# Block-diagonal 128-row aggregations replaced by pairs of 64-row matmuls in a four-layer graph network

## The chip, the cores and the metric

The kernel runs on one core of a Trainium2 chip. The metric is the device time of one execution in microseconds (us); lower is better. A core has five engines [...]: TensorE (PE; its weight loads are shown apart as PEld), VectorE (DVE), ScalarE (ACT), GpSimd (POOL) and SyncE (SP), which here only starts transfers.

## The reference

There are 128 graphs of 64 nodes with 512 features each, all in f32. Four layers run one after the other; each is a residual and a layer norm around one kind of graph network:

```python
# layer 0
y = x @ w; s = y @ a
A = s[..., :, None] + s[..., None, :]
A = jnp.tanh(A / 8.0) * 8.0
A = jnp.where(A >= 0, A, 0.1 * A)
A = jnp.exp(A) * A_shape
A = A / jnp.sum(A, axis=-1, keepdims=True)
A = A * jnp.sum(A_shape, axis=-1, keepdims=True)
out = A @ x @ w
# layer 1
weight = adj * jnp.exp(einsum('bqd,bkd->bqk', query, keyt))
weight = weight / jnp.sum(weight, axis=2, keepdims=True)
out = einsum('bqk,bkd->bqd', weight, value)
# layer 2
agg = einsum('bij,bjd->bid', adj, k * mask)
w = inv_scale * mask * einsum('bid,bid->bi', q, agg)
out = softmax(w, axis=1)[:, :, None] * v
# layer 3, twice (hidden width 1024), relu and layer norm between
m = Be[:, :, None] * einsum('nce,nch->neh', H, x @ W.T)
out = Dn[:, :, None] * einsum('nce,neh->nch', H, m) + b
# after every layer
x = layernorm(x + out)
```

`H` is 1 where the adjacency is not zero, `Be` and `Dn` are inverse sums over it. Every `A @ x`-like product mixes nodes of one graph only: a 64 x 64 matrix per graph.

## The kernel before, in words

Two graphs fill the 128 partitions of a tile; a group is two such tiles (`GT = 2`), and there are 32 groups. `run(g)` is a generator that carries one group through all four layers and yields between stages; the loop at the end of the kernel keeps four groups in flight, starts one every fourth step and advances the oldest first. The framework's scheduler then sets the order within each engine's queue, so in the middle of the run a round of about 78 us repeats, in which TensorE works on four groups at different layers: layer 3's second product for the oldest, layer 2's scores, layer 1's attention, layer 0's aggregation for the youngest.

Each group's matrix of 64 x 64 per graph is spread to a 128 x 128 block-diagonal matrix per tile. The buffers for these (`e_bd` three, `h_bd` two, `g_bd` three) are zeroed once by GpSimd at the start (L90), ahead of the weights' transfers in the same queue; after that only the two diagonal blocks are written, by `on_diagonal` (L357), L425 and L461, each with two instructions of 64 partitions. With them:

- `gathered` (L282) computes the transposed aggregate of a tile with four matmuls of 128 x 128 per tile, into one PSUM buffer `tr` (there are two), which ScalarE copies to SBUF (L289); it is called in layer 0 (with `e`) and at the start of layer 3 (with `G`). Layer 3's second aggregation does the same over 1024 columns (L502, copies L503).
- `row_sums` (L324) multiplies with a column of ones, once per tile.
- Layer 1's attention is one matmul per tile (L419), and layer 3's matrix `G` one per tile (L458).

The scores of layers 1 and 2 (L320) and the broadcast of layer 0 (L374) already run as matmuls with 128 rows and 64 columns per graph, the two graphs in turn. An f32 matmul of the source is two passes in the trace, each with its own weight load.

The weight products are `product` (L296: w0, wv1, wv2, w3a, w3b) and `product_T` (L305). `transposed` (L278) transposes `x` after a layer norm, through the same two `tr` buffers; its copies are L279. The layer norm is L342 to L346 on VectorE, with its power of -0.5 on GpSimd (L335). L389, L420, L464 and L506 add a layer's result to `x`. L402 adds a bias to `x` on GpSimd.

Of the kernel before, what the change touches and what calls it, by code (L numbers as in the profile page):

```python
# [22 lines left out]
KC = D // P  # L23
KH = DH // P
# [7 lines left out]
def kernel(  # L32
# [38 lines left out]
    ones = cpool.tile([P, 1], FP, name="ones")  # L71
# [3 lines left out]
    halves = ((slice(0, N), slice(0, N)), (slice(N, P), slice(N, P)))  # L75
# [5 lines left out]

    eye = cpool.tile([P, N], FP, name="eye")
    nc.vector.tensor_add(eye, ident[:, :N], ident[:, N:])


    def diagonals(name, n):
        made = []
        for i in range(n):
            t_ = cpool.tile([P, GT, P], FP, name=f"{name}{i}")
            nc.gpsimd.memset(t_, 0.0)  # L90
            made.append(t_)
        turn = [0]

        def take():
            turn[0] += 1
            return made[turn[0] % n]

        return take

    next_e = diagonals("e_bd", 3)  # L100
    next_h = diagonals("h_bd", 2)
    next_g = diagonals("g_bd", 3)

    x_g = x.rearrange("(g t p) d -> g p t d", t=GT, p=P)
    out_g = out.rearrange("(g t p) d -> g p t d", t=GT, p=P)
# [46 lines left out]
    w3b_sb = weights(w3b, DH, D, "w3b_sb")  # L152
# [120 lines left out]
    def transposed(xt):  # L273
        xT = work.tile([P, KC, GT * P], FP, name="xT")
        for t in range(GT):
            tr = ps_tr.tile([P, KC, P], FP, name="tr")
            for c in range(KC):
                nc.tensor.transpose(tr[:, c, :], xt[:, t, ts(c, P)], ident)  # L278
            nc.scalar.copy(xT[:, :, ts(t, P)], tr)  # L279
        return xT  # L280

    def gathered(xt, bd):  # L282

        gT = work.tile([P, KC, GT * P], FP, name="xT")
        for t in range(GT):
            tr = ps_tr.tile([P, KC, P], FP, name="tr")
            for c in range(KC):
                nc.tensor.matmul(tr[:, c, :], xt[:, t, ts(c, P)], bd[:, t, :], start=True, stop=True)  # L288
            nc.scalar.copy(gT[:, :, ts(t, P)], tr)  # L289
        return gT  # L290

    def product(lhsT, t, w, cols=slice(0, D), chunks=KC):

        ps = ps_mm.tile([P, D], FP, name="mm")
        for k in range(chunks):
            nc.tensor.matmul(ps, lhsT[:, k, ts(t, P)], w[:, k, cols], start=(k == 0), stop=(k == chunks - 1))  # L296
        return ps
# [14 lines left out]
    def scores(zT, xT):  # L312

        ps = ps_sm.tile([P, GT, P], FP, name="sm")
        for t in range(GT):

            for k in range(KC):
                for rows, cols in halves:
                    tok = slice(t * P + cols.start, t * P + cols.stop)
                    nc.tensor.matmul(ps[rows, t, :N], zT[:, k, tok], xT[:, k, tok],  # L320
                                     start=(k == 0), stop=(k == KC - 1))
        return ps[:, :, :N]

    def row_sums(bd):  # L324
        ps = ps_sm.tile([P, GT, P], FP, name="sm")
        for t in range(GT):
            nc.tensor.matmul(ps[:, t, 0:1], bd[:, t, :], ones, start=True, stop=True)  # L327
        return ps[:, :, 0]

    def rstd_of(mv):  # L330
# [7 lines left out]
    def layer_norm(xt):  # L338
        st = small.tile([P, GT, 6], FP, name="st")
        mv = small.tile([P, GT, 2], FP, name="mv")  # L340
        for t in range(GT):
            nc.vector.bn_stats(st[:, t, :], xt[:, t, :])  # L342
            nc.vector.bn_aggr(mv[:, t, :], st[:, t, :])
        rstd = rstd_of(mv)
        for t in range(GT):
            nc.vector.tensor_scalar(xt[:, t, :], xt[:, t, :], mv[:, t, 0:1], rstd[:, t : t + 1],  # L346
                                    ALU.subtract, ALU.mult)
# [6 lines left out]
    def on_diagonal(dst, e, adj):  # L354

        for rows, cols in halves:
            nc.vector.tensor_mul(dst[rows, :, cols], e[rows], adj[rows])  # L357
        return dst


    def run(g):
        xt = xs.pop(g)
        adj, bhd, am, radj, g1 = prepared[g // GC]
        own = ts(g % GC, GT)
        adj, bhd, am, radj, g1 = adj[:, own], bhd[:, own], am[:, own], radj[:, own], g1[:, own]
# [12 lines left out]
        nc.scalar.activation(e, e, AF.Tanh, scale=0.125)  # L378
        nc.vector.scalar_tensor_tensor(e, e, 0.1, e, ALU.mult, ALU.max)
        nc.scalar.activation(e, e, AF.Exp, scale=8.0)  # L380
        bd = on_diagonal(next_e(), e, adj)
        yield
        gT = gathered(xt, bd)
        f = small.tile([P, GT], FP, name="f")
        nc.vector.reciprocal(f, row_sums(bd))  # L385
        nc.vector.tensor_mul(f, f, radj)
        yield
        for t in range(GT):
# [6 lines left out]
        xT = transposed(xt)  # L395
# [9 lines left out]
        v = work.tile([P, GT, D], FP, name="z")  # L405
# [7 lines left out]
        bd = on_diagonal(next_e(), e, adj)  # L413
        yield
        f = small.tile([P, GT], FP, name="f")
        nc.vector.reciprocal(f, row_sums(bd))
        for t in range(GT):
            po = ps_mm.tile([P, D], FP, name="mm")
            nc.tensor.matmul(po, bd[:, t, :], v[:, t, :], start=True, stop=True)  # L419
            nc.vector.scalar_tensor_tensor(xt[:, t, :], po, f[:, t : t + 1], xt[:, t, :], ALU.mult, ALU.add)  # L420
        layer_norm(xt)

        h_bd = next_h()
        for rows, cols in halves:
            nc.vector.tensor_scalar(h_bd[rows, :, cols], adj[rows], 0.0, None, ALU.not_equal)  # L425
        yield


        xT = transposed(xt)
# [3 lines left out]
        ps = scores(xT, zT)  # L433
# [4 lines left out]
        ps = ps_sm.tile([P, GT, P], FP, name="sm")  # L438
# [6 lines left out]
        e = work.tile([P, GT, N], FP, name="e")  # L445
# [9 lines left out]

        pg = ps_sm.tile([P, GT, P], FP, name="sm")
        for t in range(GT):
            nc.tensor.matmul(pg[:, t, :N], h_bd[:, t, :], bhd[:, t, :], start=True, stop=True)  # L458
        gm = next_g()
        for rows, cols in halves:  # L460
            nc.scalar.copy(gm[rows, :, cols], pg[rows, :, :N])  # L461
        yield
        for t in range(GT):
            nc.vector.scalar_tensor_tensor(xt[:, t, :], product(xT, t, wv2_sb), wc[:, t : t + 1], xt[:, t, :],  # L464
# [2 lines left out]
        yield  # L467


        gT = gathered(xt, gm)  # L470

        for t in range(GT):
            c = work.tile([P, D], FP, name="junk")
# [5 lines left out]
        h = stage.tile([P, GT, DH], FP, name="h")  # L479
# [13 lines left out]
            nc.scalar.activation(h[:, t, :], h[:, t, :], AF.Identity, bias=nm[:, t : t + 1],  # L493
                                 scale=rstd[:, t : t + 1])
        yield
        ghT = []
        for t in range(GT):
            ghT.append(work.tile([P, KH, P], FP, name="ghT"))
            for i in range(KH // KC):
                tr = ps_tr.tile([P, KC, P], FP, name="tr")  # L500
                for c in range(KC):
                    nc.tensor.matmul(tr[:, c, :], h[:, t, ts(i * KC + c, P)], gm[:, t, :], start=True, stop=True)  # L502
# [73 lines left out]
```

## Time and profile before

| | |
|---|---|
| median of three runs | 2634.96 us (2633.36 to 2637.23) |
| profiled execution | 2635.76 us |
| its span | 2634.0 us |
| granted TensorE clock | 0.998 |
| VectorE / ScalarE / GpSimd busy | 1138.0 / 590.6 / 546.8 us |

The span is the time from the first to the last instruction of the profiled execution. A group of instructions is written as line, engine, operation, tiles and shape, then the count, the busy time together, the mean duration of one in nanoseconds, and the idle time of the engine just before them with what ended it. For matmuls "128*64 128x64" means 128 rows, 64 weight columns, and 64 columns streamed; a mean duration includes latency, so the spacing of starts tells more. In a timeline the columns are start, length, engine, line, operation, tiles, shape and count.

### The profile page before, as it was taken

How to read it: one execution, taken by the hardware profiler on the slowest of the kernel's cores; microseconds unless marked ns; L12 is line 12 of the kernel's file. 1: busy time of each engine (PE TensorE's matmuls, PEld its weight loads, DVE VectorE, ACT ScalarE, POOL GpSimd, SP SyncE). 2: the span in 40 equal slices, each digit the busy share in tenths (PEclk: the TensorE clock that was granted, in tenths of full speed). 3: DMA queues.
4: the chain of work that ended last, by engine and by line, in shares of the span. 5: the costliest groups of instructions: out<-in, count | busy, mean ns of one | idle time of the engine just before them, and what ended most of it. 6: DMA issues, size and time to landing. Idle time of an engine off the chain costs nothing.

```text
span 2634.0 us, 27593 instructions
## 1 busy us (share of the span) xinstructions
PE 2556.3 (97%) x11272; PEld 1544.1 (59%) x11272; DVE 1138.0 (43%) x2552; ACT 590.6 (22%) x1164; POOL 546.8 (21%) x560
## 2 busy tenths in 40 slices
PE   6999999999999999999999999999999999999998
PEld 4565565655565655565655565655665655665654
DVE  3535453445433455433545434445443445433443
ACT  0222221222221222221122221222221222221221
POOL 4211221212211222211312212212212212211211
PEclk9999999999999999999999999999999999999999
DMA  5000000000000000000000000000000000000000
GB/s 217 32 1 17 5 17 17 16 17 13 8 16 17 21 17 8 10 17 20 17 16 4 14 21 17 17 17 1 17 16 17 17 17 0 17 16 8 9 9 16
DMA packets 22190, 50.31 MB, mean 19 GB/s; under 512 B 1504, under 2 KB 1504, under 8 KB 22064
## 3 DMA queue, kind: packets, MB, share of 16 engines
q1 hardware_dynamic: 18560, 35.66, 4.0%
q0 software_dynamic: 3504, 12.89, 1.3%
q8 instruction: 89, 1.46, 0.2%
q14 instruction: 37, 0.30, 0.0%
HBM read 31.76 MB, written 16.78 MB: 18 GB/s over the span
## 4 chain that ended last, share of the span: by engine, by line
PE 87%; DVE 5%; issue 5%; POOL 3%; DMA 0%; ACT 0%; POOLq 0%; DVEq 0%
PE mm L296 57%; PE mm L305 17%; PE tr L288 4%; PE sm L320 2%; POOL rstd L335 2%; DVE x L346 2%; PE tr L278 1%; DVE x L420 1%; PE mm L169 1%; PE mm L225 1%; DVE x L389 1%; PE mm L419 1%; PE sm L327 1%; PE sm L374 0%; DMA junk<-in_a_dram 0%
## 5 line engine op out<-in xcount | busy, mean ns | idle before, releaser
L296 PE MATMUL mm<-wv_sb,xT 128*128 128x512 f32 x1024 | 460.6, 593 | 0.0
L305 PE MATMUL mm<-xT,m_sb 128*128 128x256 f32 x2048 | 458.3, 381 | 2.1 <-DVE hw L254 1.5
L296 PE MATMUL mm<-w3a_sb,xT 128*128 128x512 f32 x1024 | 448.0, 595 | 0.0
L296 PE MATMUL mm<-w3b_sb,ghT 128*128 128x512 f32 x1024 | 444.7, 592 | 0.0
L305 PEld LDWEIGHTS mm<-xT,m_sb 128*128 128x128 f32 x2048 | 385.7, 190 | 70.8 <-issue 17.9
L335 POOL TENSOR_TENSOR rstd<-ve,mhalf 128x2 f32<-128x2 f32 x160 | 127.7, 798 | 1369.9 <-DVE ve L333 1291.0
L296 PEld LDWEIGHTS mm<-w3b_sb,ghT 128*128 128x128 f32 x1024 | 194.5, 190 | 244.4 <-issue 244.4
L296 PEld LDWEIGHTS mm<-w3a_sb,xT 128*128 128x128 f32 x1024 | 191.9, 190 | 231.7 <-issue 229.6
L296 PEld LDWEIGHTS mm<-wv_sb,xT 128*128 128x128 f32 x1024 | 187.2, 190 | 185.8 <-issue 183.9
L385 DVE RECIPROCAL f<-sm 128x2 f32<-128x2 f32 x32 | 5.5, 171 | 617.9 <-PE sm L327 617.9
L296 PE MATMUL mm<-w_sb,xT 128*128 128x512 f32 x512 | 225.2, 593 | 0.4 <-issue 0.4
L346 DVE TENSOR_SCALAR x<-x,mv,rstd 128x512 f32<-128x512 f32 x256 | 185.3, 765 | 75.2 <-POOL rstd L335 75.2
L342 DVE BATCH_NORM_STATS2 st<-x 128x6 f32<-128x512 f32 x256 | 176.0, 688 | 4.7
L485 DVE TENSOR_TENSOR h<-mm,b3a_b 128x512 f32<-128x512 f32 x128 | 88.5, 692 | 193.4 <-PE mm L296 193.4
L296 PEld LDWEIGHTS mm<-w_sb,xT 128*128 128x128 f32 x512 | 97.0, 190 | 122.3 <-issue 122.2
L486 ACT ACTIVATE h<-h 128x512 f32<-128x512 f32 x128 | 80.6, 630 | 387.7 <-DVE h L485 387.7
L506 DVE TENSOR_TENSOR x<-mm,x 128x512 f32<-128x512 f32 x64 | 44.3, 691 | 277.0 <-PE mm L296 277.0
L476 POOL TENSOR_SCALAR x<-x 128x512 f32<-128x512 f32 x64 | 39.7, 620 | 559.9 <-PE tr L288 559.9
L502 PE MATMUL tr<-g_bd,h 128*128 128x128 f32 x1024 | 125.7, 282 | 5.5 <-ACT h L493 5.5
L487 DVE BATCH_NORM_STATS2 st<-h 128x6 f32<-128x512 f32 x128 | 88.8, 694 | 88.4 <-ACT h L486 88.4
L309 ACT ACTIVATE z<-mm,r_c 128x256 f32<-128x256 f32 x128 | 60.6, 473 | 293.7 <-PE mm L305 293.7
L502 PEld LDWEIGHTS tr<-g_bd,h 128*128 128x128 f32 x1024 | 121.3, 195 | 7.7 <-ACT h L493 7.4
(138 smaller groups left out, 2374.4 us busy)
## 6 DMA issues: line engine op xcount, KB each, us to landing
x<-in_x_dram SPq DMA_DIRECT2D x32, 512.0 KB, 3.7
out_dram<-x SPq DMA_DIRECT2D x32, 512.0 KB, 2.8
adj<-in_adjT_dram SPq DMA_DIRECT2D x8, 256.0 KB, 2.8
wv_sb<-in_wv_dram POOLq DMA_DIRECT2D x2, 1024.0 KB, 15.3
w3a_sb<-in_w3a_dram POOLq DMA_DIRECT2D x1, 2048.0 KB, 17.4
w3b_sb<-in_w3b_dram POOLq DMA_DIRECT2D x1, 2048.0 KB, 16.4
h<-in_wqk_dram POOLq DMA_DIRECT2D x2, 1024.0 KB, 5.7
w_sb<-in_w_dram POOLq DMA_DIRECT2D x1, 1024.0 KB, 10.7
```

The source lines that it names most:

```text
L288: nc.tensor.matmul(tr[:, c, :], xt[:, t, ts(c, P)], bd[:, t, :], start=True, stop=True)
L296: nc.tensor.matmul(ps, lhsT[:, k, ts(t, P)], w[:, k, cols], start=(k == 0), stop=(k == chunks - 1))
L305: nc.tensor.matmul(pz[:, : GT * P], w[:, k, ts(c, P)], xT[:, k, :], start=(k == 0), stop=(k == KC - 1))
L309: nc.scalar.activation(zT[:, c, :], pz[:, : GT * P], AF.Identity, bias=bias[:, c : c + 1])
L320: nc.tensor.matmul(ps[rows, t, :N], zT[:, k, tok], xT[:, k, tok], start=(k == 0), stop=(k == KC - 1))
L335: nc.gpsimd.tensor_tensor(rstd, ve, mhalf, ALU.pow)
L342: nc.vector.bn_stats(st[:, t, :], xt[:, t, :])
L346: nc.vector.tensor_scalar(xt[:, t, :], xt[:, t, :], mv[:, t, 0:1], rstd[:, t : t + 1], ALU.subtract, ALU.mult)
L485: nc.vector.tensor_add(hi, product(gT, t, w3a_sb, ts(i, D)), b3a_b[:, ts(i, D)])
L486: nc.scalar.activation(hi, hi, AF.Relu)
L487: nc.vector.bn_stats(st[:, t, i, :], hi)
L502: nc.tensor.matmul(tr[:, c, :], h[:, t, ts(i * KC + c, P)], gm[:, t, :], start=True, stop=True)
```

## The change

The block-diagonal buffers, `diagonals` and `on_diagonal` are removed. The masked matrices stay as 128 partitions x 64 columns (two graphs above each other), written by one instruction each. Every matmul that used a block-diagonal matrix becomes two, one per graph, with 64 rows: the upper graph's on partitions 0 to 63, the lower graph's on 64 to 127.

In `gathered` the two graphs' results go to two different PSUM buffers: `trs` takes both `tr` buffers at once, one per half of the partitions, each holding both tiles; the matmuls go through the feature chunks, the tiles and the halves, and two copies follow at the end, which write runs of 64 columns. The function now takes its destination and the first chunk, and layer 3's second aggregation calls it twice. `ghT` becomes one buffer for both tiles (`bufs=1`) in place of one per tile. Row sums, attention and `G` write the two halves of the partitions of one PSUM buffer. In the built program the scheduler also orders some pieces differently: the second half of layer 3's aggregation comes after one matmul of wv2, and layer 0's aggregation stands between two parts of layer 1's scores.

```diff
-    def diagonals(name, n):
-        made = []
-        for i in range(n):
-            t_ = cpool.tile([P, GT, P], FP, name=f"{name}{i}")
-            nc.gpsimd.memset(t_, 0.0)
-            made.append(t_)
...
-    def gathered(xt, bd):
-
-        gT = work.tile([P, KC, GT * P], FP, name="xT")
-        for t in range(GT):
-            tr = ps_tr.tile([P, KC, P], FP, name="tr")
-            for c in range(KC):
-                nc.tensor.matmul(tr[:, c, :], xt[:, t, ts(c, P)], bd[:, t, :], start=True, stop=True)
-            nc.scalar.copy(gT[:, :, ts(t, P)], tr)
-        return gT
+    def gathered(dst, src, chunks, e):
+
+
+        trs = [ps_tr.tile([P, KC, GT, N], FP, name="tr") for _ in halves]
+        for c in range(KC):
+            for t in range(GT):
+                for tr, (rows, cols) in zip(trs, halves):
+                    nc.tensor.matmul(tr[:, c, t, :], src[rows, t, ts(chunks + c, P)], e[rows, t, :],
+                                     start=True, stop=True)
+        for h, tr in enumerate(trs):
+            nc.scalar.copy(dst.rearrange("p c (t h n) -> p h c t n", h=2, n=N)[:, h], tr)
+        return dst
...
-    def row_sums(bd):
+    def row_sums(e):
         ps = ps_sm.tile([P, GT, P], FP, name="sm")
         for t in range(GT):
-            nc.tensor.matmul(ps[:, t, 0:1], bd[:, t, :], ones, start=True, stop=True)
+            for rows, _ in halves:
+                nc.tensor.matmul(ps[rows, t, 0:1], e[rows, t, :], ones[rows], start=True, stop=True)
         return ps[:, :, 0]
...
-        bd = on_diagonal(next_e(), e, adj)
+        nc.vector.tensor_mul(e, e, adj)
...
-            nc.tensor.matmul(po, bd[:, t, :], v[:, t, :], start=True, stop=True)
+            for rows, _ in halves:
+                nc.tensor.matmul(po[rows], e[rows, t, :], v[rows, t, :], start=True, stop=True)
...
-        h_bd = next_h()
-        for rows, cols in halves:
-            nc.vector.tensor_scalar(h_bd[rows, :, cols], adj[rows], 0.0, None, ALU.not_equal)
+        hT = work.tile([P, GT, N], FP, name="hT")
+        nc.vector.tensor_scalar(hT, adj, 0.0, None, ALU.not_equal)
...
-            nc.tensor.matmul(pg[:, t, :N], h_bd[:, t, :], bhd[:, t, :], start=True, stop=True)
-        gm = next_g()
-        for rows, cols in halves:
-            nc.scalar.copy(gm[rows, :, cols], pg[rows, :, :N])
+            for rows, _ in halves:
+                nc.tensor.matmul(pg[rows, t, :N], hT[rows, t, :], bhd[rows, t, :], start=True, stop=True)
+        gm = work.tile([P, GT, N], FP, name="gm")
+        nc.scalar.copy(gm, pg[:, :, :N])
...
-        ghT = []
-        for t in range(GT):
-            ghT.append(work.tile([P, KH, P], FP, name="ghT"))
-            for i in range(KH // KC):
-                tr = ps_tr.tile([P, KC, P], FP, name="tr")
-                for c in range(KC):
-                    nc.tensor.matmul(tr[:, c, :], h[:, t, ts(i * KC + c, P)], gm[:, t, :], start=True, stop=True)
-                nc.scalar.copy(ghT[t][:, ts(i, KC), :], tr)
-        yield
-        for t in range(GT):
-            nc.vector.tensor_add(xt[:, t, :], product(ghT[t], 0, w3b_sb, chunks=KH), xt[:, t, :])
+        ghT = work.tile([P, KH, GT * P], FP, name="ghT", bufs=1)
+        for i in range(KH // KC):
+            gathered(ghT[:, ts(i, KC), :], h, i * KC, gm)
+        yield
+        for t in range(GT):
+            nc.vector.tensor_add(xt[:, t, :], product(ghT, t, w3b_sb, chunks=KH), xt[:, t, :])
```

In the changed kernel the matmul of `gathered` stands at L270, its copies at L273, the row sums at L312, attention at L399, the product with `same` at L419, `G` at L438, the transposes at L259, the scores at L304, and the layer norm's last step at L331.

More of the change, by code (lines that the diff above doesn't have):

```diff
@@ L83 @@
     nc.vector.tensor_add(eye, ident[:, :N], ident[:, N:])
-    def diagonals(name, n):
-        made = []
-        for i in range(n):
-            t_ = cpool.tile([P, GT, P], FP, name=f"{name}{i}")
-            nc.gpsimd.memset(t_, 0.0)
-            made.append(t_)
[L92 to L102, printed above, removed]
     x_g = x.rearrange("(g t p) d -> g p t d", t=GT, p=P)
@@ L352, in row_dot @@
         nc.vector.scalar_tensor_tensor(junk, u, scale, v, ALU.mult, ALU.mult, accum_out=dst)
-    def on_diagonal(dst, e, adj):
-        for rows, cols in halves:
-            nc.vector.tensor_mul(dst[rows, :, cols], e[rows], adj[rows])
-        return dst
     def run(g):
@@ L380, in run @@
         nc.scalar.activation(e, e, AF.Exp, scale=8.0)
-        bd = on_diagonal(next_e(), e, adj)
+        nc.vector.tensor_mul(e, e, adj)
         yield
-        gT = gathered(xt, bd)
+        gT = gathered(work.tile([P, KC, GT * P], FP, name="xT"), xt, 0, e)
         f = small.tile([P, GT], FP, name="f")
-        nc.vector.reciprocal(f, row_sums(bd))
+        nc.vector.reciprocal(f, row_sums(e))
         nc.vector.tensor_mul(f, f, radj)
@@ L412, in run @@
             nc.scalar.activation(e[:, t, :], ps[:, t, :], AF.Exp, bias=d[:, t : t + 1])
-        bd = on_diagonal(next_e(), e, adj)
+        nc.vector.tensor_mul(e, e, adj)
         yield
         f = small.tile([P, GT], FP, name="f")
-        nc.vector.reciprocal(f, row_sums(bd))
+        nc.vector.reciprocal(f, row_sums(e))
         for t in range(GT):
             po = ps_mm.tile([P, D], FP, name="mm")
-            nc.tensor.matmul(po, bd[:, t, :], v[:, t, :], start=True, stop=True)
+            for rows, _ in halves:
+                nc.tensor.matmul(po[rows], e[rows, t, :], v[rows, t, :], start=True, stop=True)
             nc.vector.scalar_tensor_tensor(xt[:, t, :], po, f[:, t : t + 1], xt[:, t, :], ALU.mult, ALU.add)
         layer_norm(xt)
-        h_bd = next_h()
-        for rows, cols in halves:
-            nc.vector.tensor_scalar(h_bd[rows, :, cols], adj[rows], 0.0, None, ALU.not_equal)
+        hT = work.tile([P, GT, N], FP, name="hT")
+        nc.vector.tensor_scalar(hT, adj, 0.0, None, ALU.not_equal)
         yield
@@ L457, in run @@
         for t in range(GT):
-            nc.tensor.matmul(pg[:, t, :N], h_bd[:, t, :], bhd[:, t, :], start=True, stop=True)
-        gm = next_g()
-        for rows, cols in halves:
-            nc.scalar.copy(gm[rows, :, cols], pg[rows, :, :N])
+            for rows, _ in halves:
+                nc.tensor.matmul(pg[rows, t, :N], hT[rows, t, :], bhd[rows, t, :], start=True, stop=True)
+        gm = work.tile([P, GT, N], FP, name="gm")
+        nc.scalar.copy(gm, pg[:, :, :N])
         yield
@@ L467, in run @@
         yield
-        gT = gathered(xt, gm)
+        gT = gathered(work.tile([P, KC, GT * P], FP, name="xT"), xt, 0, gm)
         for t in range(GT):
```

## The prediction

> **What bounds the kernel now.** First the page: busy time by engine, slices, chain of waits.
>
> ```profile
> PE 2556.3 (97%) x11272; PEld 1544.1 (59%) x11272; DVE 1138.0 (43%) x2552; ACT 590.6 (22%) x1164; POOL 546.8 (21%) x560
> ...
> PE   6999999999999999999999999999999999999998
> ...
> PEclk9999999999999999999999999999999999999999
> ...
> PE 87%; DVE 5%; issue 5%; POOL 3%; DMA 0%; ACT 0%; POOLq 0%; DVEq 0%
> ```
>
> TensorE is the bound in every slice, at full clock; no other engine is half busy. So the change is worth what it does to TensorE's issue time and to the few holes in it; the savings on VectorE and ScalarE count only where TensorE waits for them. Second, the groups by form. A matmul of the source is two rows here (two f32 passes: 32 groups x 16 matmuls at L502 give x1024).
>
> ```profile
> L502 PE MATMUL tr<-g_bd,h 128*128 128x128 f32 x1024 | 125.7, 282 | 5.5 <-ACT h L493 5.5
> L278 PE MATMUL tr<-ident,x 128*128 128x128 f32 x512 | 77.9, 276 | 41.6 <-DVE x L346 41.6
> L288 PE MATMUL tr<-e_bd,x 128*128 128x128 f32 x512 | 65.9, 283 | 2.1 <-issue 2.1
> L288 PE MATMUL tr<-g_bd,x 128*128 128x128 f32 x512 | 63.3, 275 | 0.0
> ```
>
> The only hole of size is 41.6 us at L278, 1.3 us a round of the pipeline. Third, the TensorE timeline of one round, for the steps from start to start (means are latencies and overlap).
>
> ```profile
> 1333.84 0.50 PE L327 MATMUL sm<-ones,e_bd 128*128 128x1 f32 x4
> 1334.20 1.96 PE L419 MATMUL mm<-z,e_bd 128*128 128x512 f32 x4
> 1336.00 0.38 PE L440 MATMUL sm<-e,same 128*128 128x128 f32 x2
> 1336.22 0.56 PE L458 MATMUL sm<-bhd,h_bd 128*128 128x64 f32 x4
> 1336.62 3.84 PE L502 MATMUL tr<-g_bd,h 128*128 128x128 f32 x32
> 1340.29 0.60 PE L278 MATMUL tr<-ident,x 128*128 128x128 f32 x4
> 1340.73 1.02 PE L296 MATMUL mm<-wv_sb,xT 128*128 128x512 f32 x2
> 1341.59 0.60 PE L278 MATMUL tr<-ident,x 128*128 128x128 f32 x4
> 1344.10 0.63 PE L278 MATMUL tr<-ident,x 128*128 128x128 f32 x4 [1.91 <-DVE x L346]
> ...
> 1390.17 1.15 PE L320 MATMUL sm<-xT,z 128*64 128x64 f32 x32
> 1391.15 1.10 PE L320 MATMUL sm<-z,xT 128*64 128x64 f32 x32
> ```
>
> L502 steps (1340.29 - 1336.62) / 32 = 0.115 us a pass; L458, with half the columns to stream, still 0.10 to 0.11, and so does L327 with one column: these are bound by loading 128 columns of weights. The scores of L320, two column tiles in turn, take 0.98 us for 32 passes: 0.058 us a pair, so both tiles load and stream at once.
>
> [...] The last L296 pass starts at 1364.43 and the first L374 at 1364.95: 0.52 against 0.43 us between passes, plus a first pass of 270 instead of 222 ns: 0.14 us to enter a mode with 64 weight columns. Leaving L320 for w3a: 1391.15 to 1392.18 is 1.03 us against 16 x 0.058 = 0.93, and the next w3a pass comes 0.54 instead of 0.43 us later: 0.20 us to enter one with 128. [...]
>
> **The change part by part**, per round of about 78 us.
>
> 1. Aggregations (L288 twice, L502). Before: 64 passes of 0.112 us. After: 128 passes, each loading 128 columns from 64 rows. If the two row tiles overlap as the two column tiles do, a pair takes 0.112 us: the same time. Taken at 0, and not below, since the load of 128 columns sets the pair; if the tiles do not overlap, +0.112 us a pair (rival 1).
>
> 2. Row sums (twice) and G: 64 columns to load, in tile pairs. Each goes from 4 x 0.112 = 0.45 us to 4 x 0.058 = 0.23: -0.65 us together. Attention (L419): 8 passes in pairs of 0.43 us for 4 of 0.43: 0.
>
> 3. Modes. Before, a round has two excursions (L374, L320), four switches. In the built order of the changed kernel it has fifteen: the row sums and attention (64x64), L440 (128x128), G (64x64), first h gather (64x128), a wv2 matmul, second h gather, wv2 again, later the gm gather, row sums, seven scores, the e gather, the other scores. Eleven are new. By the two measured prices, less 0.06 us where a gather is left [...]: five at 0.20, four at 0.14, two at 0.09: +1.75 us. Between 0 [...] and 0.25 each.
>
> 4. PSUM turns. A gather now holds both tr buffers to its end, where before the second tile's matmuls covered the first's copy. A copy starts about 0.31 us after the last pass of its burst starts (eighth pass of L288 at 1386.12 + 7 x 0.112 = 1386.90, copy at 1387.21), takes 0.59, and TensorE resumes 0.13 later (a copy of L279 ends at 1345.35, the load behind it starts at 1345.48): first buffer back after 1.03 us, second after about 1.5. The built order meets this by running one half alone: four matmuls of half 0, four of half 1, then in turn, for the e gather; two and two for the second h gather. Alone they don't pair: 8 + 4 periods of 0.112 us more, +1.35 us. The wv2 matmul and the scores in between (over 1 us) hide the rest of the copies; were they not there, another 0.3 to 0.5 us a gather would show. [...] Between 0.3 and 1.6 us.
>
> 5. The hole at L278. The wait is for VectorE's second layer norm, queued behind the first. In the changed order the second h gather and one more wv2 matmul stand ahead, and with the switches these transposes come about 11.5 us after the last w0 pass, where VectorE, counted as before, is done after 10.2 (last w0 pass 1333.41; the second pair of L346 starts at 1342.48 and takes 2 x 0.54 undisturbed); the GpSimd bias add that slowed L346 (L402) starts only after the first group's transposes. So it goes: 2.1 us in the round shown by starts (1342.03 to 1344.10), on average 1.3 + 0.2 + 0.1 (a late pass at 1345.5) = -1.6 us. Next in line is ScalarE's copy of the first group's transposes, ready about 0.2 us early. Between -1.6 and 0.
>
> 6. VectorE and ScalarE: two masked products become one per call, L425 (2 x 0.87 us) becomes one L404, two G copies one. VectorE is hidden under TensorE except at L278, counted above: 0.
>
> 7. Ends. Eight memsets of 0.3 us leave POOL's queue ahead of the first weight DMA; TensorE first waits for that queue's second transfer (16.0 us idle): -2.4 us once, or 0 if the transfers bound it. At the tail the last h gather has nothing beside it: lone halves and two late copies, +1.5 us. In 7 rounds the gm gather is cut by a stretch of L305: two more switches of 0.20, +2.8 us in all.
>
> Sum per round: -0.65 + 1.75 + 1.35 - 1.6 = +0.85 us; 30 full rounds +25.5, ends +1.9: +27 us. The profiled execution took 2635.76 us (span 2634.0), which gives 2663; the median of the runs, 2634.96, gives **2662 us**.
>
> **Rivals.** (1) Row tiles don't overlap. For: the trace has no 64-row matmul at all, and each half's two f32 passes could be issued back to back. Against: the column tiles overlap, loads and both passes included. Pairs per round 16 + 8 + 16 + 12 = 52; x 0.112 = +5.8 us, x 31 = +180: 2842 us, near 2895 if attention (+1.72 a round) serialises too. (2) Faster: [...] Each of the eleven new switches enters or leaves a 64-row form; for it: the measured switches change the column split only. At zero for all, -1.75 x 30 = -52: 2610 us. It decides from the point where a new switch costs 0.08 us on average instead of 0.16 (27 / 30 / 11). [...] (3) No change: half of the switch cost, or a stagger of 0.5 us, 2635. (4) Worse holes: the stall stays because the copies, not VectorE, are late: +1.6 x 30 = 48, 2710.
>
> **How the numbers follow.** This kernel can be told from no change from about 0.2% (5.3 us). Forecast with its own range 2641 to 2690: 0.42. Rival 4: 0.10. Rival 1, full or in part: 0.15. Slower together 0.67. No change 0.11. Faster 0.22. The range: rival 2 in full gives 2610; above, rival 4 with a third of rival 1 (48 + 60) gives 2770. Left out are full serialisation (0.12) and what is faster still (0.05).
>
> **What would show it.** L270: pair steps of 0.112 us confirm step 1, 0.224 rival 1. First passes after a change of form 0.1 to 0.2 us late confirm step 3. Idle at L259 for VectorE near 0 confirms step 5; idle at L270 or L259 for ScalarE above 0.5 us a round is rival 4. The e gather should last about 2.7 us, the gm gather 1.8. First TensorE work at 13.6 us confirms step 7. The prediction is wrong if L270 passes neither pair nor serialise, or if switches are free.

## The result and the profile after

The changed kernel takes **2652.48 us** (median of four runs, 2650.85 to 2653.01) against 2634.16 us for the kernel before on the same chip (2632.34 to 2637.23): a ratio of 1.0067, 95% interval 1.005 to 1.0085, so 18.3 us slower. The profiled execution took 2652.37 us, with a span of 2650.5 against 2634.0.

The page of the changed kernel: busy time, granted clock and chain of waits.

```profile
PE 2612.4 (99%) x13832; PEld 1549.1 (58%) x13832; DVE 1056.3 (40%) x2456; ACT 572.6 (22%) x1132; POOL 538.6 (20%) x552
...
PEclk9999999999999999999999999999999999999998
...
PE 97%; issue 1%; DVE 1%; DMA 0%; ACT 0%; POOL 0%; POOLq 0%; DVEq 0%
```

TensorE's share of the chain of waits rose from 87% to 97%, and VectorE and GpSimd, which had 8% of it, have 1%: the waits for the layer norm are gone from all full rounds, and still the kernel is slower. VectorE has 82 us less work (1138.0 to 1056.3); 53 us of it lie in the last step of the layer norm, which does the same work in less time (185.3 to 132.0; see under Buffers). The groups by form, TensorE alone:

```profile
L270 PE MATMUL tr<-gm,h 64*128 64x64 f32 x2048 | 138.6, 280 | 6.1 <-ACT h L472 5.4 <-ACT ghT L273 0.7
L270 PE MATMUL tr<-e,x 64*128 64x64 f32 x1024 | 80.1, 281 | 1.7 <-DVE e L360 1.7
L259 PE MATMUL tr<-ident,x 128*128 128x128 f32 x512 | 66.7, 273 | 3.9 <-DVE x L331 3.9
L270 PE MATMUL tr<-gm,x 64*128 64x64 f32 x1024 | 66.6, 276 | 0.0
```

The wait for VectorE ahead of the transposes fell from 41.6 to 3.9 us. The gathers go by what they read: the e gather is layer 0's, the gm gather stands at the start of layer 3 (tiles gm and x), and the two h gathers are layer 3's second aggregation. The gm gather has twice the passes (x1024 for x512) in almost the same busy time, 66.6 for 63.3 us; the e gather, with the same number of passes, needs 80.1. The TensorE timeline of one round says why:

```profile
1311.81 0.40 PE L312 MATMUL sm<-ones,e 64*64 64x1 f32 x8
1312.13 0.68 PE L304 MATMUL sm<-xT,z 128*64 128x64 f32 x14
1312.74 2.50 PE L270 MATMUL tr<-e,x 64*128 64x64 f32 x32
1315.17 0.74 PE L304 MATMUL sm<-xT,z 128*64 128x64 f32 x17
...
1337.62 0.40 PE L312 MATMUL sm<-ones,e 64*64 64x1 f32 x8
1337.88 1.91 PE L399 MATMUL mm<-z,e 64*64 64x512 f32 x8
1339.72 0.49 PE L419 MATMUL sm<-e,same 128*128 128x128 f32 x2
1340.14 0.45 PE L438 MATMUL sm<-bhd,hT 64*64 64x64 f32 x8
1340.52 2.00 PE L270 MATMUL tr<-gm,h 64*128 64x64 f32 x32
1342.45 1.13 PE L280 MATMUL mm<-wv_sb,xT 128*128 128x512 f32 x2
1343.51 2.17 PE L270 MATMUL tr<-gm,h 64*128 64x64 f32 x32
1345.60 1.12 PE L280 MATMUL mm<-wv_sb,xT 128*128 128x512 f32 x2
1346.56 1.04 PE L259 MATMUL tr<-ident,x 128*128 128x128 f32 x8
```

Three things are to be seen. From start to start the first h gather takes 1342.45 - 1340.52 = 1.93 us for 16 pairs: 1.79 us at 0.112 us a pair and a first pass 0.14 us late, so the two row tiles (the upper and the lower 64 rows) do overlap. The second h gather takes 2.09 and the e gather 2.43 us: in both, passes of one half run alone. And no line ends in an idle time: the 2.1 us that stood here before the transposes are covered. A round, from one w3a to the next, takes 78.67 us in place of 78.28. After every fourth group the kernel prepares the matrices of the next four, a chunk: the six such rounds behind the first w3a take 82.66 us for 81.93, and the round after one 78.67 for 79.06.

Of the 16.5 us between the two spans, these rounds leave the changed kernel only 8.4 us behind at the w3a of group 28 (2426.23 us from the span's start against 2417.86). The other 8.1 us come at the end, where no other group fills TensorE. The TensorE timeline of the last aggregation, kernel before:

```profile
2605.68 6.71 PE L502 MATMUL tr<-g_bd,h 128*128 128x128 f32 x32 [4.93 <-ACT h L493]
2612.22 13.90 PE L296 MATMUL mm<-w3b_sb,ghT 128*128 128x512 f32 x32
```

and the same of the changed kernel:

```profile
2616.99 0.69 PE L270 MATMUL tr<-gm,h 64*128 64x64 f32 x4 [4.93 <-ACT h L472]
2618.13 3.25 PE L270 MATMUL tr<-gm,h 64*128 64x64 f32 x28 [0.44 <-ACT h L472]
2622.05 5.01 PE L270 MATMUL tr<-gm,h 64*128 64x64 f32 x32 [0.67 <-ACT ghT L273]
2626.99 16.09 PE L280 MATMUL mm<-w3b_sb,ghT 128*128 128x512 f32 x32
```

From the first pass to w3b it takes 10.0 us instead of 6.5, and w3b itself lasts 16.09 us instead of 13.90. TensorE's granted clock is at half from 2604.90 to 2611.72 us in the kernel before, and from 2614.17 to 2631.23 us in the changed one.

### The profile page after: what moved, and what is told of

Read it like the earlier page. It is cut to its first block, busy times and chain, and to the rows that moved or that the text cites. A ratio compares the mean times of both kernels' runs of the same rounds, so it can differ in the third digit from the quotient of the medians.

```text
span 2650.5 us, 32538 instructions
## 1 busy us (share of the span) xinstructions
PE 2612.4 (99%) x13832; PEld 1549.1 (58%) x13832; DVE 1056.3 (40%) x2456; ACT 572.6 (22%) x1132; POOL 538.6 (20%) x552
## 3 DMA queue, kind: packets, MB, share of 16 engines
q8 instruction: 109, 1.79, 0.3%
## 4 chain that ended last, share of the span: by engine, by line
PE 97%; issue 1%; DVE 1%; DMA 0%; ACT 0%; POOL 0%; POOLq 0%; DVEq 0%
PE mm L280 58%; PE mm L289 17%; PE tr L270 10%; PE sm L304 3%; PE mm L399 2%; PE tr L259 2%; PE mm L150 1%; PE mm L206 1%; PE sm L312 1%; PE sm L419 0%; PE sm L353 0%; PE sm L438 0%; DMA junk<-in_a_dram 0%; PE sm L169 0%; DVE junk L337 0%
## 5 line engine op out<-in xcount | busy, mean ns | idle before, releaser
L280 PE MATMUL mm<-wv_sb,xT 128*128 128x512 f32 x1024 | 474.1, 601 | 0.0
L331 DVE TENSOR_SCALAR x<-x,mv,rstd 128x512 f32<-128x512 f32 x256 | 132.0, 558 | 75.8 <-POOL rstd L320 75.7
L270 PEld LDWEIGHTS tr<-gm,h 64*128 64x128 f32 x2048 | 129.2, 192 | 35.9 <-ACT ghT L273 24.4
L270 PE MATMUL tr<-gm,h 64*128 64x64 f32 x2048 | 138.6, 280 | 6.1 <-ACT h L472 5.4
```

What stands on the lines that cost most here:

```text
L270: nc.tensor.matmul(tr[:, c, t, :], src[rows, t, ts(chunks + c, P)], e[rows, t, :], start=True, stop=True)
```

## The experiments

**Small matmuls alone, gathers alone.** The change in two parts, on the kernel before: `small64` makes the row sums, the attention and `G` 64-row matmuls on the diagonal blocks; `gather64` makes only the aggregations so, with the two `tr` buffers by halves as in the change.

```diff
-            nc.tensor.matmul(pg[:, t, :N], h_bd[:, t, :], bhd[:, t, :], start=True, stop=True)
+            for rows, cols in halves:
+                nc.tensor.matmul(pg[rows, t, :N], h_bd[rows, t, cols], bhd[rows, t, :], start=True, stop=True)
...
+        trs = [ps_tr.tile([P, KC, GT, N], FP, name="tr") for _ in halves]
...
+                    nc.tensor.matmul(tr[:, c, t, :], src[rows, t, ts(chunks + c, P)], e[rows, t, cols],
+                                     start=True, stop=True)
```

> The kernel before, but row sums, attention and G as 64-row matmuls on the two diagonal blocks of the same block-diagonal buffers; aggregations stay at 128 rows; the queue order is unchanged. Theory (mode switches and holes decide): a round saves 0.60 us of matmul time and pays five new switches, 0.115 + 0.19 + 0.145 + 0.20 + 0.115 = 0.77 us; what falls ahead of the transposes is absorbed by the hole there, so the time stays within 5 us of before and the idle time at the transposes for VectorE falls from 41.6 us to about 34. Rival (small products are where 64 rows pay): 0.60 us a round, about 18 us faster than before.

> The kernel before, but the four aggregations in two 64-row halves as in the changed kernel, on the diagonal blocks of the block-diagonal buffers; row sums, attention and G stay at 128 rows. Theory: a round pays eight new switches (1.3 us) and 0.65 us in which one half runs alone, and wins 1.4 us by the hole at the transposes: +0.5 us a round, and about 7 us in the tail, so 18 to 26 us slower than before, a little slower than the changed kernel; VectorE idle at the transposes near 0. Rival (the 64-row gathers cost nothing and the small products' switches are the loss): within 5 us of before.

Measured: `small64` 2633.42 us beside 2633.95 (ratio 0.9998, 0.999 to 1.0006), an ordinary round 78.21 us; `gather64` 2662.55 us (1.0116, 1.0101 to 1.0132), an ordinary round 78.77 us. So the small matmuls give nothing by themselves: what they save goes into the switches into and out of their form. The gathers alone cost 28.6 us, more than the 18 to 26 that were expected, and close the hole alone: the wait for VectorE is 4.2 us in `gather64`, none of it in a full round, and 33.0 in `small64`. By ordinary rounds the parts add up, +0.49 and -0.07 us against +0.39 for the whole. By the medians they don't, 28.1 us against 18.3, and the profiled executions show where: `gather64` is 3.4 us later than the changed kernel at the first w3a (202.85 us), loses 13.4 us and not 9.3 over the 28 rounds behind it, of which 1.5 come from one round in which the granted clock fell to half for 3.41 us, and takes 2.0 us longer from the w3a of group 28 to the end. By the prices read in the trace (below), `gather64` has 1.31 us of new switches a round; with 0.65 for lone halves and -1.38 for the hole that makes +0.58, and its round is longer by 0.49.

**VectorE in halves.** The changed kernel, with the three masked operations on VectorE again done in two instructions of 64 partitions.

```diff
-        nc.vector.tensor_mul(e, e, adj)
+        for rows, _ in halves:
+            nc.vector.tensor_mul(e[rows], e[rows], adj[rows])
...
```

> The changed kernel, but the masked products and the not-equal matrix written again by two VectorE instructions of 64 partitions each, as before the change; TensorE's order is that of the changed kernel. Theory (the hole at the transposes closed because more matmuls stand ahead of it): within 4 us of the changed kernel, no new idle at the transposes. Rival (it closed because VectorE got lighter by 0.9 us a round or more): the hole comes back, up to 1.4 us a round, 20 to 40 us slower than the changed kernel.

Measured: 2653.29 us (1.0071, 1.0059 to 1.0084), the same rounds of 78.67 and 82.66 us, the wait ahead of L259 still 3.9 us. So it is not these three lighter operations that closed the hole.

**The hole closed another way.** The kernel before, with layer 2's transposes one step of the group's generator later, so that the wv2, w3b and wv1 products of other groups stand ahead of them while the layer norm runs.

```diff
+        yield
         xT = transposed(xt)
-        yield
         zT = product_T(xT, m2_sb)
```

> The kernel before with all its 128-row matmuls; only the transposes of layer 2 move from one step of the group's generator to the next, so that they stand behind wv1's products in TensorE's queue. Theory (the hole is a matter of order alone, worth 1.4 to 1.6 us a round): 2588 to 2600 us, about 1.5 percent faster than before, idle at the transposes for VectorE near 0. Rival (VectorE's chain is what bounds there and the wait moves to the next user, or the copies of the transposes become late): 2625 to 2640 us, with a new wait at the layer-2 products.

Measured: 2602.84 us (0.9881, 0.9868 to 0.9895), 1.0 us a round where 1.4 to 1.6 were expected. TensorE no longer waits at L278 at all, but this order cuts the scores and the gm gather in two, which takes 0.4 us more a round. TensorE's timeline of `yield2`, the same place in the round:

```profile
1320.79 0.60 PE L278 MATMUL tr<-ident,x 128*128 128x128 f32 x4
1321.23 1.02 PE L296 MATMUL mm<-wv_sb,xT 128*128 128x512 f32 x2
1322.09 0.60 PE L278 MATMUL tr<-ident,x 128*128 128x128 f32 x4
```

The second group's transposes, which ended the wait, have left this place. So the change's one gain can be had without its cost. The next run asks whether the change is then worth anything: `after_yield2` is the changed kernel with the same edit.

> The changed kernel with the same move of layer 2's transposes by one step as in the run yield2. Theory (the change costs 1.7 us of switches and 0.65 us of lone halves a round, saves 0.6 us on small products, and its other gain was only the hole that this move closes anyway): 2655 to 2672 us, that is 52 to 70 us above yield2, and no gain over the changed kernel. Rival (the change costs 18 us wherever it is put, and closing the hole is an independent gain): 2615 to 2628 us.

Measured: 2697.94 us (1.026, 1.0237 to 1.0284), 95 us over `yield2`; an ordinary round takes 80.04 us for 77.28. The expected 2655 to 2672 was missed on the high side. Its TensorE timeline holds the reason:

```profile
1485.20 1.10 PE L270 MATMUL tr<-gm,x 64*128 64x64 f32 x8
1486.23 7.17 PE L289 MATMUL mm<-xT,m_sb 128*128 128x256 f32 x32
1493.34 2.00 PE L270 MATMUL tr<-gm,x 64*128 64x64 f32 x24
```

In this order the gm gather is cut in two (probably because the moved transposes, just ahead of it, hold the `tr` buffers; no run isolates that), and both pieces enter and leave their form: 1.03 + 1.92 us from start to start for what takes 1.93 in one piece. Steps 2, 3 and 4 of the prediction at their measured sizes make +1.73 us a round where there is no hole to close; the rounds differ by 2.76, and the cut's 1.0 us is of the size of the rest.

**The price of a switch.** Two kernels on the one before: at the start of each of the four w3a products of a group, `sw64` puts one pair of 64x64 matmuls, and `sw128`, as a control, one 128-row matmul with as many passes in time. The results are overwritten by the product that follows.

```diff
+        for rows, c64 in halves if w is w3a_sb else ():
+            nc.tensor.matmul(ps[rows, :N], ident[rows, c64], ident[rows, c64], start=True, stop=True)
...
+        if w is w3a_sb:
+            nc.tensor.matmul(ps[:, :N], ident, ident[:, :N], start=True, stop=True)
```

> The kernel before with a pair of small 64-row matmuls (64 x 64, identity blocks, result overwritten at once) put ahead of each of the four w3a products of a group: 8 switches more a group. Theory [...]: 0.12 us of matmuls and 0.34 us of switching each, 4 x 32 x 0.46 = 58 us slower than before. Rival (switching to a row-tiled form is free): 4 x 32 x 0.12 = 15 us slower, less than the control sw128.

> The control to sw64: at the same four places one 128-row matmul with the same number of columns, so no change of form. Both theories: two passes bound by a load of 128 columns, 4 x 32 x 0.22 = 28 us slower than before.

Measured: `sw64` 2688.21 us (1.0205, 1.0191 to 1.0219), +54.8 us beside 2633.39; `sw128` 2663.84 us (1.0113, 1.0099 to 1.0127), +30.5. Over 128 calls that is 0.428 us for `sw64`, of which the two pairs of passes take 2 x 0.058; the switch in and out costs 0.31 us. The control costs 0.238 us, its two passes of 0.112 and 0.01 more. So here it is the change of form that costs, 0.31 us, and not the interruption, 0.01.

**Buffers.** `after_tr4` and `after_tr3` are the changed kernel with four and three PSUM buffers for transposed results instead of two; the products then have two and three instead of four, so that the sum of all PSUM buffers stays at eight.

```diff
-    ps_mm = ctx.enter_context(tc.tile_pool(name="ps_mm", bufs=4, space=bass.MemoryType.PSUM))
-    ps_tr = ctx.enter_context(tc.tile_pool(name="ps_tr", bufs=2, space=bass.MemoryType.PSUM))
+    ps_mm = ctx.enter_context(tc.tile_pool(name="ps_mm", bufs=2, space=bass.MemoryType.PSUM))
+    ps_tr = ctx.enter_context(tc.tile_pool(name="ps_tr", bufs=4, space=bass.MemoryType.PSUM))
```

> The changed kernel with four buffers for the gathers' results and two for the products, in place of two and four, so that a gather need not wait for the copies of the one before; the queue order goes back to whole gathers, with nothing between the two h gathers and no split of the scores, and the layer-2 transposes again early. Theory: lone halves gone (-0.65 us a round), four switches fewer (-0.6), but the hole at the transposes for VectorE comes back with 1.2 to 1.4 us a round: 2640 to 2650 us, 3 to 12 below the changed kernel, with idle at the transposes of 30 us or more. Rival (the buffers' turn was the main loss and the hole stays closed): 2615 to 2632 us. If two product buffers are too few, idle shows at the weight products and the time is above 2655.

> The changed kernel with three buffers for transposed results and three for products (two and four before). Theory: a gather then waits for one late copy instead of two, so that the halves that run alone (0.65 us a round) shrink to 0.2 to 0.4 us; what this frees comes back in part as TensorE's wait for VectorE ahead of the transposes of L259, as with four buffers: ordinary rounds 78.4 to 79.0 us; with three product buffers the chunk rounds stall less than with two (89.4 us): 83 to 86. Total 2645 to 2685 us. Rival: with three buffers the two halves come free at different times in another order and the halves run alone as before: rounds at 78.7 us, the wait for VectorE near 4 us as in the changed kernel, total above 2652 by the chunk rounds alone.

Measured: 2716.62 us with four (1.0313, 1.0299 to 1.0327) and 2710.61 with three (1.0289, 1.0275 to 1.0303); both missed. With four the six chunk rounds grew to about 89.4 us, which makes 40 of the 64 us over the changed kernel. In each TensorE waits 3.41 us for VectorE at a product of the preparation, so two product buffers are too few, as the expectation had feared; and then its granted clock is at half for 6.83 us, by an estimate up to 3.4 us more (half of the 6.83). For the lone halves the ordinary part of its TensorE timeline is what counts:

```profile
1387.53 3.79 PE L270 MATMUL tr<-gm,h 64*128 64x64 f32 x64
1391.25 1.09 PE L259 MATMUL tr<-ident,x 128*128 128x128 f32 x8
...
1394.90 0.63 PE L259 MATMUL tr<-ident,x 128*128 128x128 f32 x4 [1.70 <-DVE x L331]
1396.31 0.63 PE L259 MATMUL tr<-ident,x 128*128 128x128 f32 x4 [0.78 <-DVE x L331]
```

Both h gathers run as one stretch of 32 pairs, 3.72 us to the next start, with no lone half and without two switches; and with this the wait for VectorE is back, 54.5 us in all. An ordinary round saves 0.65 + 0.34 us by that and waits 1.55: +0.56, where these rounds grew by 0.50. The round after a chunk waits 2.48: +1.49, where it grew by 1.42. What closes the hole in the changed kernel is therefore that the transposes come later, behind the lone halves, the second wv2 matmul and the switches. The delays that cost are also what covers the wait.

The same order also takes GpSimd's bias add off VectorE's back. Before, that addition starts behind the first group's transposes and runs beside the layer norm's last step for the second group, the very step for which TensorE waits:

```profile
1342.41 2.67 POOL L402 TENSOR_TENSOR x<-x,bv_b 128x512 f32<-128x512 f32 x2
1342.48 2.88 DVE L346 TENSOR_SCALAR x<-x,mv,rstd 128x512 f32<-128x512 f32 x2 [0.58 <-POOL rstd L335]
```

In the changed kernel the step is done before the addition starts:

```profile
1346.28 1.00 DVE L331 TENSOR_SCALAR x<-x,mv,rstd 128x512 f32<-128x512 f32 x2 [0.58 <-POOL rstd L320]
1347.25 2.51 POOL L381 TENSOR_TENSOR x<-x,bv_b 128x512 f32<-128x512 f32 x2 [1.01 <-PE tr L259]
```

Beside the addition one step takes 1.47 us instead of 0.54, so about 0.9 of the 1.91 us that TensorE waited in this round were VectorE's slower step. Steps of over 1 us number 60 of 256 in the kernel before and 66 in `after_tr4`, which have the hole, and three in the changed kernel, `gather64` and `dve_halves`, which don't; `yield2` has 60, where nobody waits for them.

Three buffers gave neither gain: rounds without a chunk take between 79.2 and 82.5 us. The two h gathers take 4.60 us to the next start, because passes of the second run alone again, 0.11 us apart. The spread of the rounds is in the main the clock's: twelve times between the first w3a and that of group 28 it fell to half, mostly for 3.41 us, which costs about 1.5 us by an estimate from `gather64` (1.5 us for one such fall); and in the rounds after a chunk TensorE waits 1.6 us for VectorE.

**The end of the run.** `after_warm` is the changed kernel with six matmuls whose result nobody reads ahead of the last group's second aggregation.

```diff
+        if g == NG - 1:
+            warm = ps_mm.tile([P, D], FP, name="mm")
+            for _ in range(6):
+                nc.tensor.matmul(warm, ident, w3b_sb[:, 0, :], start=True, stop=True)
```

> The changed kernel with six matmuls of 128x512 into a product buffer that nobody reads, ahead of the last group's second aggregation. They fill the wait of 4.93 us before it, so that TensorE's granted clock does not fall there. Theory: the last 95 us lost 7 to 8 us more than the predicted 1.5 because the narrow matmuls after this wait, with gaps between them, run at half the clock for longer than the 128-row ones did (10.0 us for the last aggregation against 6.5, 16.09 us for the w3b after it against 13.90). Then the aggregation takes 4 to 6 us and w3b 13.9: 2644 to 2648 us, 4 to 8 us below the changed kernel. Rival: the aggregation is long because it waits for ScalarE's copies of its two buffers (idle 0.44 and 0.67 us), clock or no clock: then w3b may fall to 13.9 but the aggregation stays near 9 to 10 us, and the time is 2650 to 2653 us.

Measured: 2651.67 us (1.0064, 1.0052 to 1.0077): no gain that can be told. TensorE's timeline and, after it, its windows (window, length, busy time and count, granted clock, share and rate of the DMA):

```profile
2610.34 5.31 PE L478 MATMUL mm<-w3b_sb,ident 128*128 128x512 f32 x12
2615.58 0.44 PE L270 MATMUL tr<-gm,h 64*128 64x64 f32 x4
2616.56 1.78 PE L270 MATMUL tr<-gm,h 64*128 64x64 f32 x28 [0.54 <-ACT h L472]
2619.01 4.86 PE L270 MATMUL tr<-gm,h 64*128 64x64 f32 x32 [0.67 <-ACT ghT L273]
```

```profile
2616.00:2618.00 2.00, 1.46 (x28) 1.00 0.00 0
...
2620.00:2622.00 2.00, 2.00 (x17) 0.50 0.03 8
...
2630.00:2632.00 2.00, 2.00 (x6) 1.00 0.00 0
```

The wait is filled and the aggregation starts at full clock (1.00); then the clock falls within it to 0.50, and stays there into w3b. Neither theory fits: the aggregation takes 8.2 us, between the two, and w3b 16.79. The aggregation has two gaps, of 0.54 and 0.67 us, but other traces have falls without any gap. One of the falls of `after_tr3`, the gathers in TensorE's timeline and two windows, up to the fall and behind it:

```profile
1044.60 4.88 PE L270 MATMUL tr<-gm,h 64*128 64x64 f32 x64
```

```profile
1045.50:1048.91 3.41, 3.41 (x51) 1.00 0.02 5
1048.92:1052.32 3.40, 3.40 (x12) 0.50 0.00 0
```

The 3.41 us before this fall hold 64-row passes alone, and TensorE is never idle in them. So it is, in most cases with other small matmuls among them, ahead of 14 more falls of `after_tr3` and of the one in the middle of `gather64`. And it is the same on the way up. The last aggregation of `after_tr4`, where four buffers leave no gap in it, and then that of the kernel before:

```profile
2685.40 7.37 PE L270 MATMUL tr<-gm,h 64*128 64x64 f32 x64 [4.93 <-ACT h L472]
```

```profile
2688.71:2692.12 3.41, 3.41 (x35) 0.50 0.02 5
2692.12:2695.53 3.41, 3.41 (x11) 0.50 0.00 0
```

```profile
2608.31:2611.72 3.41, 3.41 (x18) 0.50 0.00 0
2611.72:2615.00 3.28, 3.28 (x13) 1.00 0.00 0
```

But for the first and the last one of a run, the stretches at half clock in these traces last 3.41 us or a multiple of it. In the kernel before, one such step filled with 128-row passes (2608.31 to 2611.72 us) is followed by the full clock, 1.00. In `after_tr4` one filled with 64-row passes (2688.71 to 2692.12) is followed by 0.50 again; there the clock rises only at 2695.53, behind a step that w3b fills but for its first 0.6 us.

**Both ends on the better order.** `y2_warm_late` is `yield2` with the same six matmuls and with the zeroing of the block-diagonal buffers behind the first five transfers of GpSimd's queue.

> The best version so far, which is the kernel before with layer 2's transposes one step later in each group (2602.84 us), with two additions at its ends: the zeroing of the block-diagonal buffers comes after GpSimd's first five weight transfers instead of ahead of them, and the six filler matmuls stand ahead of the last group's second aggregation. The theory from the changed kernel's start (TensorE began 3.3 us earlier, 0.9 us of it were left at the first w3a) and end says 1 to 3 us from the start and 2 to 3 us from the last aggregation (6.08 us at the lower clock to 3.6): 2597 to 2601 us. Rival: the transfers themselves bound the start, and the fillers only fill: 2602 to 2604 us.

Measured: **2597.82 us** (0.9866, 0.9851 to 0.9881), the fastest of all and without the change. In its profile the first w3a comes 1.5 us earlier than in `yield2` (196.26 for 197.75), and the way from the last w3a to the last w3b is 2.2 us shorter. The first of these lies within what equal starts differ by (below), and the intervals of the two ratios overlap; the second lies where the filler stands. TensorE's timeline there:

```profile
2562.96 5.31 PE L498 MATMUL mm<-w3b_sb,ident 128*128 128x512 f32 x12
2568.11 3.83 PE L505 MATMUL tr<-g_bd,h 128*128 128x128 f32 x32
2571.78 8.75 PE L295 MATMUL mm<-w3b_sb,ghT 128*128 128x512 f32 x20
```

With 128 rows the tiles take turns with their copies, the aggregation has no gap, and the granted clock is 1.00 from 2562 to 2586 us, through filler, aggregation and w3b: 3.7 us to the next start, where the 64-row form at the same place took 8.2.

## Why the prediction was right, and where its sizes were not

The direction and the mechanism held: no less work for TensorE, new switches and lone halves against a hole closed. 2662 us were forecast, 2652.5 came. The round, term by term, with the sizes from the changed kernel's timeline:

| step | forecast, us a round | measured |
|---|---|---|
| 1 aggregations as pairs | 0 | 0 (0.112 us a pair) |
| 2 row sums, G | -0.65 | -0.60 |
| 3 switches | +1.75 | +1.68 |
| 4 PSUM turns | +1.35 | +0.65 |
| 5 hole | -1.6 | -1.38 |
| sum | +0.85 | +0.35; by the starts of rounds +0.39 |

- Step 1: held; rival 1 (no overlap, 2842 us and more) is out. The gathers' weight loads of 128 columns take as long from 64 rows as from 128, 187 to 192 ns (L270) for 192 to 195 (L288 and L502 before), and the loads of 64 columns in row sums, `G` and scores 133 to 138; that 64 rows would not shorten it was an assumption when the step was put at 0. The attention's pairs of 512 columns also cost about what one 128-row pass did, 0.46 for 0.45 us, with both halves in one PSUM buffer.
- Step 2: by the spacing of passes nearly as worked out, but the prediction took 0.45 us for row sums of which its own line shows 0.36 (1333.84 to 1334.20 us); 0.26 stand there now. How much falls to this step and how much to step 3 is good to 0.1 us only; it is worth nothing without neighbours of the same form (`small64`).
- Step 3: held, and this is what rival 2, with the new switches at no cost, denied. The sum of the late first passes is 1.68 us: 0.115 into a 64x64 form from a 128-row product or a gather, 0.14 into a gather, 0.19 to 0.20 out to 128 columns. The 0.06 us taken off where a gather is left was an estimate of the author's. `sw64` against its control gives 0.31 us for a way in and out, against 0.34 by the prediction's prices.
- Step 4: the term that was mis-sized, 0.65 us instead of 1.35. The e gather lost 0.49 us and not 0.9, the second h gather 0.16 and not 0.45. The prediction read the built order as the order of execution: four source matmuls (eight passes) alone at either end of the e gather. In the trace the second half's first pass comes at 1313.24, 0.50 us after the first half's 1312.74, when five of its eight leading passes have started; the other three pair with the second half, which runs alone at the end for four passes. ScalarE's copies that clear the two `tr` buffers for it, in this round and in the next:

```profile
1311.73 1.07 ACT L273 COPY xT<-tr 128x512 f32<-128x512 f32 x2 [0.93 <-PE tr L270]
1390.58 1.07 ACT L273 COPY xT<-tr 128x512 f32<-128x512 f32 x2 [1.55 <-PE tr L270]
```

The later copy ends 0.07 us after the gather's first pass in the one (1312.81) and 0.24 us after it in the other (1391.66, first pass 1391.42), yet the second half starts 0.50 us after the first in both, and in all 29 e gathers from 195 us on. So here the order sets the stagger, at four passes instead of eight, and not the copy. In the second h gather, with four leading passes, the order would hold nothing back by the same reckoning; there the second half starts 0.17 us after the first, 0.05 us after its copy ends.
- Step 5: held, the slower step of VectorE beside the bias add included. Per ordinary round the hole was worth 1.38 us, 2.1 in those after a chunk. ScalarE's copy, named as next in line, did not come late: no idle time at L270 or L259 is put down to it in a full round.
- Step 6: held (`dve_halves`).
- Step 7: at the start TensorE began at 12.73 us, 3.3 us earlier (2.4 forecast), but at the first w3a 0.9 us of it were left. Even this is not firm, as two kernels with the same start differ there by 1.6 us (197.87 in `after_warm`, 199.46 in the changed kernel, whose clock fell to half for 3.41 us at 166.81). The chunk rounds' extra 0.4 us came as 0.34. The tail is the second mis-sized term: +8.1 us against 1.5. It counted lone halves and two late copies and left out the clock. Of the 8.1, 2.9 lie in the rounds with fewer groups in flight, 3.5 in the last aggregation, 2.2 in w3b at half clock, less 0.5 after it.

So that the forecast came within 10 us is in part luck, two errors of opposite sign: the rounds were 17 us too dear (9.3 us measured over the 28 rounds from the first w3a to that of group 28, against 28 x 0.85 + 6 x 0.4 = 26.2), and the ends 8.1 us too cheap (-0.9 and +8.1 against -2.4 and +1.5). The clock, which the prediction left out, makes the 2.2 us in w3b and a part of the 3.5 before it. What stays open is which trait of the 64-row passes went with the half clock, the fewer rows or the 64 columns that each streams where a 128-row pass streams 128.

## What to carry to other kernels

Replacing a zero-padded 128-row matmul by two 64-row ones on separate row tiles saved TensorE nothing where 128 weight columns were loaded (0.112 us a pair for 0.112 to 0.115 a pass); passes got cheaper only where the loaded columns halved too (row sums and `G`, -0.60 us a round), and each excursion into another form cost about 0.3 us (0.31 in `sw64`), so neighbours should share it. The gathers that hold both their PSUM buffers to the end did not cover their copies, 0.65 us a round; the tiles in turn, as before, did, and so did four buffers. At the end of the kernel, where nothing else fills TensorE, such matmuls also went with half clock for longer, 17.06 us for 6.82. And where a change closes a wait by coming later, try the order alone first: here one moved line was worth 31 us, and the change on top of it cost 95 us, a cut gather included.

## What the hardware showed that was not expected

- Row tiles run apart from each other inside one queue: in 29 e gathers a pass of the second half started while three passes of the first, which stand ahead of it in the order, were still to start (step 4). So a lead of eight passes in the order became one of four in time.
- The granted clock. In both kernels it is 0.50 when the last aggregation starts, after 4.93 us of waiting. In the kernel before it came back about 6 us after the aggregation began, at the end of the first whole step of 3.41 us that 128-row passes filled (2611.72 us). With 64-row passes it did not go so: in `after_tr3` TensorE was busy with them without a gap for 3.41 us, and the clock fell from 1.00 to 0.50 behind them; in `after_tr4` it was busy with them for 3.41 us at 0.50, and the next 3.41 us were at 0.50 too. Not every stretch of small passes ends so: in the changed kernel gathers, row sums and scores ran from 1388.55 to 1395.50 us at 1.00. Whether the gaps of 0.54 and 0.67 us had a part in the fall of `after_warm` no run shows.
- VectorE's last step of the layer norm (L331) takes 558 ns on average where the same instruction (L346) took 765 in the kernel before. No operand changed; in the new order GpSimd's bias add no longer runs beside it (1.47 us with it, 0.54 without). In the kernel before TensorE waits for that slower step; in `yield2`, with 766 ns on average, nothing does.
